# The last group of a four-layer graph network: where its copies and activations run, and how its last rows are written

## The chip, the core and the metric

The kernel runs on one core of one Trainium2 chip. A core has TensorE (PE, with its weight loads shown as PEld), VectorE (DVE), ScalarE (ACT), GpSimd (POOL), SyncE (SP, which only issues transfers here) and 16 DMA engines. Each engine takes its own instructions in order; they wait for each other by semaphores. The metric is the device time of one execution in microseconds, the median of several runs. All arithmetic is in float32.

## The reference, cut to what matters

The input is 128 graphs of 64 nodes with 512 features: `x` (128, 64, 512), `adj` (128, 64, 64), and a node mask. Four layers follow one another, each as `x = layernorm(x + layer(x))`:

```python
# layer 0: hypergraph convolution twice, with H = (adj != 0) and row weights Dn, Be
m   = Be * (H^T @ (x @ W^T));   conv = Dn * (H @ m) + b
h   = layer_norm(relu(conv(x, W1, b1))) * gamma + beta;   y = conv(h, W2, b2) + x
# layer 1: a rank-one attention
s   = (x @ w) @ a;   A = s[i] + s[j];   A = tanh(A / 8) * 8;   A = where(A >= 0, A, 0.1 * A)
A   = exp(A) * adj;  A = A / A.sum(-1) * adj.sum(-1);   y = A @ x @ w
# layer 2: three graph convolutions
x1  = relu(adj @ (x @ W1) + b1);   x2 = relu(adj @ (x1 @ W2) + b2);   y = adj @ (x2 @ W3) + b3
# layer 3: attention with 8 heads of 64, plus terms in adj
attn = softmax(masked(q @ k^T / 8)) * 0.33 + 0.33 * adj + 0.33 * exp(-adj)   # under the mask
y   = (attn @ v) @ W_out + b_out
```

The output is `x` after layer 3.

## The kernel before

**Tiling.** Two graphs make a *pair* of 128 rows, two pairs a *duo*, and four pairs a *group* of 512 rows: the 8192 rows are 16 groups. A group's features sit in `xg` (128 partitions, 4 pairs, 512). Where a product needs features on the partitions, the group is held transposed in a `Left` (128, 4 chunks, 512 rows).

**Products.** `multiply` computes a 512x512x512 product in four quadrants from seven products of half size instead of eight. `Left.sums` makes the three sums or differences of quadrants that this takes on the left side (DVE, L518 to L521). The seven products (`product`, all recorded as L539) accumulate in three tiles named `a_...`, `b_...` and `c_...`. Between them ACT copies intermediate sums away (`snap`, L555), DVE adds quadrants together (L575, L581, L590), and ACT copies the last quadrant (L600). `rows_of` is the plain product for one pair, written to a tile `pp`; it is used by the first group, and by the last one for the output projection. Accumulators come from `ps_acc` (4 banks), all other PSUM tiles (`gth`, `xtp`, `ptp`, `agg`) from `ps_gt` (4 banks).

**Order.** The lists `start`, `order`, `step_1`, `step_last` and `rest_last` at the end of the kernel give the order of the stages. In the steady part three groups are interleaved: `a` (layers 0 and 1) of one group, `b` (layer 2 and the scores of layer 3) of the group before, `t` (the rest of layer 3) of the one before that. In `step_last` only `b` of the last group (q = 15, `NGRP - 1`) and `t` of group 14 are left, and in `rest_last` only `t` of the last group, `last_rows`. Within this order a scheduler places the instructions of each engine; `behind(key)` keeps an instruction after a named one, `in_turn(engine)` after the newest one of that engine. In `rest_last` PE and DVE are kept strictly in the written order (those instructions are recorded under L127, the helper's line).

**The last group's stages, in order of time.**

- `l2a`: the first layer-2 product. Its quadrants land in `h1` (named `aT_h` in the profile); the relu with bias is L1081 (by quadrants, in `relu`, group 0) or L1089 (by chunks of 128x512, all later groups). `pv` of group 14 (L1376) and its copies `taken` (L1388, to `aT_oT`) fall between `l2a` and `l2b`.
- `l2b`, then `gth` (L1112), which multiplies with the adjacency and leaves `h2` transposed in four `ps_gt` banks; eight relus (L1120) bring it to SBUF. `shifted` adds the bias `gb3` to `xg` (L737) and makes the masks (`prepare_masks`, L719 to L730) on DVE. Then `h2.sums()` and `l2c`.
- the aggregation `agg` (L1145), a layer norm, and `xtp` (L1165), which transposes `xg` into PSUM; four copies (L1170) bring it to `aT_xT`, and the products `q`, `k` follow.
- `last_rows`: softmax steps, `ptp` (the probabilities transposed), `pv`, `taken`, and for each pair `projected` (the product `pp`), `added` (to `xg`), `layer_norm` and a write. Pair 3 is done in two halves of 256 columns in one PSUM tile. Writes are issued by SP (L1262 for pairs 0 to 2, L1288 for pair 3).

Weights stream through a ring of 20 tiles, issued by SP as places come free.

Of the kernel before, what the change touches and what calls it, by code (L numbers as in the profile page):

```python
# [8 lines left out]
FP = mybir.dt.float32  # L9
U8 = mybir.dt.uint8  # L10
AF = mybir.ActivationFunctionType
ALU = mybir.AluOpType
AX = mybir.AxisListType

P = 128
C = 64
D = 512
# [4 lines left out]
KD = D // P  # L22
Q = 256
# [3 lines left out]
LA = LD = LG = 0.33  # L27
# [14 lines left out]
def kernel(  # L42
# [28 lines left out]
    nc = tc.nc  # L71
    NT = x.shape[0]
    NPAIR = NT // P
    NGRP = NPAIR // G
# [370 lines left out]
    def rstd(mv, n, key, at=slice(None)):  # L445
        rs = small.tile([P, n], FP, name=f"rs_{key}", tag="rs")
        act.activation(rs[:, at], mv[:, at, 1], AF.Sqrt, bias=eps_t)  # L447
        vec.reciprocal(rs[:, at], rs[:, at])
        return rs
# [48 lines left out]
    def newest(engine):  # L498
        return next(i for i in reversed(nc.cur_bb.bb.instructions) if i.engine == engine)
# [112 lines left out]
    def turned(t):  # L612

        return lambda m, n: t[:, 2 * n : 2 * n + 2, m * Q : (m + 1) * Q]
# [118 lines left out]
    def shifted(g, key):  # L733

        with behind(key):
            for p in range(G):
                vec.tensor_add(g["x"][:, p, :], g["x"][:, p, :], gb3_bc)  # L737
            prepare_masks(g)
# [147 lines left out]

    def rows_of(p, ts, quads, u0=0, u1=None, ps=None, ns=range(2)):

        if ps is None:
            ps = ps_acc.tile([P, 2, Q], FP, name=f"pp_{p}", tag="acc")  # L890
        us = range(len(ts))[u0:u1]
        for n in ns:
            for u in us:
                for c in range(KD):
                    ten.matmul(
                        ps[:, n, :], ts[u][:, c, p * P : (p + 1) * P], quads[u][c // 2, n][:, c % 2],
                        start=(n == 0 and u == 0 and c == 0), stop=(u == len(ts) - 1 and c == KD - 1),
                        skip_group_check=True,
                    )
        return ps  # L900
# [162 lines left out]
    def second_half(g):  # L1063
# [18 lines left out]
                    turned(h1.t)(m, n)[:, c], src[:, c], AF.Relu, bias=gb1_col[:, 2 * n + c : 2 * n + c + 1]  # L1082
                )

        for _ in multiply([left], (w_g[0], q), turned(h1.t), f"l2a_{q}", flipped=True, then=relu if q == 0 else None):
            yield "l2a1"
        if q > 0:
            for c in range(KD):
                act.activation(h1.t[:, c, :], h1.t[:, c, :], AF.Relu, bias=gb1_col[:, c : c + 1])  # L1089
        h1.sums()  # L1090
# [5 lines left out]
        adt = grp.tile([P, G, C], FP, name=f"adt_{q}", tag="adt", bufs=1)  # L1096
        act.activation(adt, g["atc"], AF.Exp, scale=-1.0)
        g["adt"] = adt
        if alone:
            shifted(g, f"l2b_{q}")  # L1100
        yield "gb3"

# [2 lines left out]
        for c2 in range(2):  # L1105
            ps = [ps_gt.tile([P, 2, G, C], FP, name=f"gth2_{q}_{c2}_{h}", tag="gt") for h in range(2)]
            for c in range(2):
                for p in range(G):
                    for f in range(2):
                        for h in range(2):  # L1110
                            rows, c0 = slice(h * C, (h + 1) * C), (2 * c2 + c) * P + f * C
                            ten.matmul(  # L1112
                                ps[h][f * C : (f + 1) * C, c, p, :],
                                g2[rows, p, c0 : c0 + C], g["atc"][rows, p, :], start=True, stop=True,
                            )
            for c in range(2):
                k = 2 * c2 + c
                o = h2.t[:, k, :].rearrange("p (d h t) -> p d h t", d=2, h=2)
                for h in range(2):
                    act.activation(  # L1120
                        o[:, :, h, :], ps[h][:, c].rearrange("p (d a) i -> p d (a i)", d=2),
                        AF.Relu, bias=gb2_col[:, k : k + 1],
                    )
        if not alone:
            shifted(g, f"l0w2_{q + 1}.u2")
        h2.sums()
        yield "gh"
        g3 = big.tile([P, G, D], FP, name=f"g3_{q}", tag="big")
        gen = multiply([h2], (w_g[2], q), nat(g3), f"l2c_{q}", stops=(3, 5),
# [28 lines left out]
        for duo in range(2):  # L1158
            ps = [ps_gt.tile([P, KD, 2, C], FP, name=f"xtp_{q}_{duo}_{h}", tag="gt") for h in range(2)]
            for c in range(KD):  # L1160
                for p in range(2):
                    for h in range(2):
                        rows = slice(h * C, (h + 1) * C)
                        with behind("l1w_1.p6") if q == 0 else nullcontext():
                            ten.transpose(  # L1165
                                ps[h][:, c, p, :], xg[rows, 2 * duo + p, c * P : (c + 1) * P], identc[rows]
                            )
            o = left.t[:, :, duo * Q : (duo + 1) * Q].rearrange("p c (a g i) -> p c a g i", a=2, g=2)
            for h in range(2):
                act.copy(o[:, :, :, h, :], ps[h])  # L1170
        left.sums()
        yield "xT"
        qT = big.tile([P, KD, T], FP, name=f"qT_{q}", tag="big")
# [50 lines left out]
    def last_rows(g, probs, v, left):  # L1224

        q, xg = g["q"], g["x"]
        o = out[q * T : (q + 1) * T, :].rearrange("(p t) d -> t p d", t=P)
        gen = multiply([left], (w_v, q), nat(v), f"v_{q}", stops=(3, 6))
        next(gen)
        yield "v1"  # L1230
        steps = [[softmax_steps(g, duo, probs[duo], h2) for h2 in range(2)] for duo in range(2)]
        for n in range(2):
            for h2 in range(2):
                next(steps[0][h2])
        for n in range(2):
            next(steps[1][0])
        for h2 in range(2):
            next(steps[0][h2])
        next(gen)
        yield "v2"  # L1240
        left = Left(f"oT_{q}")
        pts = turn_probs(g, 0, probs[0])
        whole(gen)
        yield "v"
        taken(0, attend(g, 0, pts, v), left)
        for n in range(2):
            next(steps[1][1])
        for h2 in range(2):
            next(steps[1][h2])
        yield "pv0"  # L1250

        def projected(p, ps=None, n=None):
            return rows_of(p, [left.t], stream.here[w_o, q], ps=ps, ns=range(2) if n is None else (n,))

        def added(p, ps, n=None):
            cols = slice(0, D) if n is None else slice(n * Q, (n + 1) * Q)
            row = xg[:, p, cols]
            vec.tensor_add(row, ps.rearrange("p n f -> p (n f)")[:, cols], row)

        def written(p):  # L1260
            layer_norm(xg, f"l3_{q}_{p}", (p,))
            nc.sync.dma_start(out=o[:, p], in_=xg[:, p])  # L1262

        ps = projected(0)
        pts = turn_probs(g, 1, probs[1])
        added(0, ps)
        written(0)
        yield "o1"
        ps = projected(1, n=0)
        taken(1, attend(g, 1, pts, v), left)  # L1270
        ps = projected(1, ps, n=1)
        added(1, ps)
        written(1)
        yield "pv1"
        added(2, projected(2))
        written(2)

        st = small.tile([P, 2, 6], FP, name="st_last", tag="st_last", bufs=1)
        ps = None
        for n in range(2):  # L1280
            ps = projected(3, ps, n=n)
            added(3, ps, n)
            vec.bn_stats(st[:, n], xg[:, 3, n * Q : (n + 1) * Q])
        mv = small.tile([P, 1, 2], FP, name="mv_last", tag="mv_last", bufs=1)
        vec.bn_aggr(mv[:, 0, :], st.rearrange("p n s -> p (n s)"))
        rs = rstd(mv, 1, "last")
        vec.tensor_scalar(xg[:, 3], xg[:, 3], mv[:, 0, 0:1], rs[:, 0:1], ALU.subtract, ALU.mult)
        nc.sync.dma_start(out=o[:, 3], in_=xg[:, 3])  # L1288
        yield "o"

    def softmax_steps(g, duo, ds, h2):
# [73 lines left out]
    def attend(g, duo, pts, v):  # L1365

        q = g["q"]

        ps = [ps_acc.tile([P, 4, 2, C], FP, name=f"pv_{q}_{duo}_{gg}", tag="acc") for gg in range(2)]
        for hc in range(4):  # L1370
            for p in range(2):
                for h2 in range(2):
                    hd = 2 * hc + h2
                    for gg in range(2):
                        rows = slice(gg * C, (gg + 1) * C)
                        ten.matmul(  # L1376
                            ps[gg][h2 * C : (h2 + 1) * C, hc, p, :],
                            v[rows, 2 * duo + p, hd * C : (hd + 1) * C],
                            pts[p][rows, h2 * 4 + hc, :],
                            start=True,  # L1380
                            stop=True,
                        )
        return ps

    def taken(duo, ps, left):
        o4 = left.t[:, :, duo * Q : (duo + 1) * Q].rearrange("p c (a g i) -> p c a g i", a=2, g=2)
        for gg in range(2):
            act.mul(o4[:, :, :, gg, :], ps[gg], LA)  # L1388

# [174 lines left out]
```

## Time and profile before

| | |
|---|---|
| median of 3 runs | 2749.85 us (2749.43 to 2751.62) |
| the profiled execution | 2749.3 us |
| its span, first to last instruction | 2747.5 us |
| granted TensorE clock, mean | 0.999 of full speed |
| busy: PE, DVE, ACT, POOL | 2722.5, 2079.6, 803.3, 38.1 us |
| last group alone (`rest_last`, from the first v product at 2708.8) | 38.7 us |
| longest kinds of wait on ACT | for DVE's statistics: 244.2 us in 44 waits |

An idle engine costs time only where the chain that ends last passes through it. So the head of the page says which engine carries that chain, the chain of waits says where it leaves that engine, and the timeline around such a place says which instruction was late. The profiled execution is one of many; its durations are read from it, and its own time is set beside the median of the runs.

### The profile page before, as it was taken

Reading aid. Unit: us, or ns where it says so; the run is one execution under the profiler, and the core shown is the slowest. Engines: PE = TensorE matmul, PEld = TensorE weight load, DVE = VectorE, ACT = ScalarE, POOL = GpSimd, SP = SyncE. Lnnn points to the kernel's source line nnn. Section 1 sums busy time; section 2 is a strip of 40 time slices with the busy share of each in tenths; the row PEclk is TensorE's granted clock in tenths of the full one; section 3 lists DMA queues with packets and bytes.
Section 4 is the critical chain, followed back from the end, with each engine's and each line's share of the span. In section 5 each row is a group of like instructions: output and inputs, shape, how many; then the busy total and the mean of one; then the engine's idle time right before and its main releaser. Section 6 shows DMA issues by size and latency. Waiting matters only on the chain.

```text
span 2747.5 us, 67717 instructions
## 1 busy us (share of the span) xinstructions
PE 2722.5 (99%) x28770; PEld 2347.5 (85%) x28770; DVE 2079.6 (76%) x4117; ACT 803.3 (29%) x1444; POOL 38.1 (1%) x71
## 2 busy tenths in 40 slices
PE   9999999999999999999999999999999999999998
PEld 7878888888888888888888888888888888888887
DVE  6878687776877778777786877778777687776766
ACT  3323323233232322322223232232322323232232
POOL 2000000000000000000000000000000000000000
PEclk9999999999999999999999999999999999999999
DMA  8535454454544545445454454545545455454441
GB/s 264 179 107 164 129 166 140 141 165 131 171 132 138 167 132 165 131 143 167 130 167 131 143 165 131 165 126 153 159 131 170 129 159 147 130 163 132 151 124 61
DMA packets 309388, 405.14 MB, mean 147 GB/s; under 512 B 57408, under 2 KB 185184, under 8 KB 309088
## 3 DMA queue, kind: packets, MB, share of 16 engines
q1 hardware_dynamic: 304256, 385.58, 47.5%
q0 software_dynamic: 4832, 15.24, 1.5%
q8 instruction: 228, 3.74, 0.6%
q14 instruction: 72, 0.59, 0.1%
HBM read 369.78 MB, written 30.93 MB: 146 GB/s over the span
## 4 chain that ended last, share of the span: by engine, by line
PE 88%; DVE 10%; ACT 1%; issue 1%; POOL 0%; DVEq 0%; POOLq 0%
PE a_l0w L539 13%; PE b_l0w L539 7%; PE a_l2b L539 4%; PE a_q L539 4%; PE a_k L539 4%; PE a_l2a L539 4%; PE a_v L539 4%; PE c_l0w L539 4%; PE a_l1w L539 4%; PE gt_l L481 3%; PE a_wo L539 3%; PE gt_l0h L481 2%; PE a_l2c L539 2%; PE b_l2b L539 2%; PE b_q L539 2%; PE b_k L539 2%
## 5 line engine op out<-in xcount | busy, mean ns | idle before, releaser
L539 PE MATMUL a_l0w<-w2w,aT_l0h 128*128 128x256 f32 x720 | 164.3, 381 | 0.0
L457 DVE BATCH_NORM_STATS2 st_l<-x 128x6 f32<-128x512 f32 x244 | 157.4, 671 | 0.6
L539 PEld LDWEIGHTS a_l0w<-w2w,aT_l0h 128*128 128x128 f32 x720 | 135.6, 190 | 18.8
L463 DVE TENSOR_SCALAR x<-x,mv_l,rs_l 128x512 f32<-128x512 f32 x244 | 119.2, 541 | 2.2
L539 PE MATMUL b_l0w<-w2w,s_l0h 128*128 128x256 f32 x480 | 108.5, 379 | 0.0
L771 ACT ACTIVATE h<-h 128x1024 f32<-128x1024 f32 (+1 forms) x58 | 54.9, 947 | 178.5 <-DVE h L590 157.5
L539 PEld LDWEIGHTS b_l0w<-w2w,s_l0h 128*128 128x128 f32 x480 | 91.1, 190 | 12.5
L1120 ACT ACTIVATE aT_h<-gth,gb_col 128x256 f32<-128x256 f32 x128 | 48.4, 489 | 159.0 <-PE gth L1112 159.0
L492 ACT COPY aT_l<-gt_l 128x512 f32<-128x512 f32 x148 | 78.1, 597 | 56.8 <-PE gt_l L481 56.8
L447 ACT ACTIVATE rs_l<-mv_l,eps_t 128x4 f32<-128x4 f32 (+1 forms) x64 | 19.0, 297 | 255.9 <-DVE mv_l L458 244.2
L555 DVE TENSOR_TENSOR u_l0w<-a_l0w,b_bc 128x512 f32<-128x512 f32 x56 | 38.6, 688 | 69.3 <-PE a_l0w L539 69.3
L539 PE MATMUL a_l2c<-gwcw,aT_h 128*128 128x256 f32 x360 | 86.7, 384 | 4.2 <-ACT u_l2c L555 3.2
L539 PE MATMUL a_l2b<-gwbw,aT_h 128*128 128x256 f32 x360 | 86.6, 383 | 0.7 <-ACT aT_oT L1388 0.7
L539 PE MATMUL a_q<-aT_xT,wqw 128*128 128x256 f32 x360 | 85.1, 379 | 0.6 <-ACT aT_xT L1170 0.6
L539 PE MATMUL a_l1w<-ww,aT_l 128*128 128x256 f32 x360 | 85.1, 379 | 0.2 <-ACT aT_l L492 0.2
L539 PE MATMUL a_k<-aT_xT,wkw 128*128 128x256 f32 x360 | 85.0, 379 | 0.0
L539 PE MATMUL a_l2a<-aT_l,gwaw 128*128 128x256 f32 x360 | 85.0, 379 | 0.0
L539 PEld LDWEIGHTS a_l2c<-gwcw,aT_h 128*128 128x128 f32 x360 | 67.0, 190 | 18.7 <-ACT u_l2c L555 8.7
L539 PE MATMUL a_v<-wvw,aT_xT 128*128 128x256 f32 x336 | 80.8, 383 | 0.0
L539 PE MATMUL a_l0w<-w1aw,aT_l 128*128 128x256 f32 x336 | 80.8, 383 | 0.0
L539 PE MATMUL a_wo<-wow,aT_oT 128*128 128x256 f32 x336 | 79.5, 379 | 0.1
L539 PE MATMUL a_l0w<-w1bw,aT_l 128*128 128x256 f32 x336 | 79.4, 379 | 0.0
(528 smaller groups left out, 6486.9 us busy)
## 6 DMA issues: line engine op xcount, KB each, us to landing
w2w<-w2k SPq DMA_DIRECT2D x210, 256.0 KB, 2.6
x<-in_x_dram SPq DMA_DIRECT2D x15, 1024.0 KB, 9.8
w1aw<-w1ak SPq DMA_DIRECT2D x60, 256.0 KB, 2.7
w1bw<-w1bk SPq DMA_DIRECT2D x60, 256.0 KB, 2.7
ww<-wk SPq DMA_DIRECT2D x60, 256.0 KB, 2.8
gwaw<-gwak SPq DMA_DIRECT2D x60, 256.0 KB, 3.1
gwbw<-gwbk SPq DMA_DIRECT2D x60, 256.0 KB, 2.6
gwcw<-gwck SPq DMA_DIRECT2D x60, 256.0 KB, 2.7
```

The lines of the kernel that those rows point to most:

```text
L447: act.activation(rs[:, at], mv[:, at, 1], AF.Sqrt, bias=eps_t)
L457: vec.bn_stats(st, xg[:, p, :])
L463: vec.tensor_scalar(xg[:, p, :], xg[:, p, :], mv[:, p, 0:1], rs[:, p : p + 1], ALU.subtract, ALU.mult)
L481: ten.matmul(ps[g][f * C : (f + 1) * C, c, p, :], src(2 * duo + p)[rows, c0 : c0 + C], mat[rows, 2 * duo + p, :], start=True, stop=True,)
L492: act.copy(o[:, :, :, g, :], ps[g])
L539: ten.matmul(acc[:, blk, :], lhsT, rhs, start=(first and blk == 0 and i == 0), stop=(last and i == n_k - 1), skip_group_check=True,)
L555: last_add[f"{key}.{what}"] = (act.copy(t, ps) if res is None else vec.tensor_add(t, ps, res(m, n))).ins
L771: act.activation(hn, hn, AF.Relu)
L1120: act.activation(o[:, :, h, :], ps[h][:, c].rearrange("p (d a) i -> p d (a i)", d=2), AF.Relu, bias=gb2_col[:, k : k + 1],)
```

## The change

All of it acts on the last group only (`q == NGRP - 1`).

- The relus of `l2a` go by quadrants, as in group 0; the last quadrant goes from PSUM through the relu without a copy of its own.
- Of the eight relus of `gth`, the four with h = 1 go to DVE as a `tensor_scalar` (add, max). `h2.sums()` comes before `shifted`.
- Of the four copies of the transposed x, two go to DVE.
- For duo 0 of `pv`, one of the two copies goes to DVE, and both come before the next softmax step. That step is split: its maximum comes before them, the subtraction and the exponential after.
- Pair 3 has a PSUM tile for each half, and both halves are multiplied at once. The statistics of pair 2 and pair 3 are written out by hand: the add and statistics of half 0 stand before the reciprocal of pair 2. Pair 3 is scaled and written in two halves, the first issued by SP, the second by ACT.

```diff
--- before.py
+++ after.py
@@ -886,7 +886,8 @@
 
     def rows_of(p, ts, quads, u0=0, u1=None, ps=None, ns=range(2)):
 
-        if ps is None:
+        fresh = ps is None
+        if fresh:
             ps = ps_acc.tile([P, 2, Q], FP, name=f"pp_{p}", tag="acc")
         us = range(len(ts))[u0:u1]
         for n in ns:
@@ -894,7 +895,7 @@
                 for c in range(KD):
                     ten.matmul(
                         ps[:, n, :], ts[u][:, c, p * P : (p + 1) * P], quads[u][c // 2, n][:, c % 2],
-                        start=(n == 0 and u == 0 and c == 0), stop=(u == len(ts) - 1 and c == KD - 1),
+                        start=(fresh and n == ns[0] and u == 0 and c == 0), stop=(u == len(ts) - 1 and c == KD - 1),
                         skip_group_check=True,
                     )
         return ps
@@ -1082,9 +1083,9 @@
                     turned(h1.t)(m, n)[:, c], src[:, c], AF.Relu, bias=gb1_col[:, 2 * n + c : 2 * n + c + 1]
                 )
 
-        for _ in multiply([left], (w_g[0], q), turned(h1.t), f"l2a_{q}", flipped=True, then=relu if q == 0 else None):
+        for _ in multiply([left], (w_g[0], q), turned(h1.t), f"l2a_{q}", flipped=True, then=relu if alone else None):
             yield "l2a1"
-        if q > 0:
+        if not alone:
             for c in range(KD):
                 act.activation(h1.t[:, c, :], h1.t[:, c, :], AF.Relu, bias=gb1_col[:, c : c + 1])
         h1.sums()
@@ -1096,7 +1097,7 @@
         adt = grp.tile([P, G, C], FP, name=f"adt_{q}", tag="adt", bufs=1)
         act.activation(adt, g["atc"], AF.Exp, scale=-1.0)
         g["adt"] = adt
-        if alone:
+        if q == 0:
             shifted(g, f"l2b_{q}")
         yield "gb3"
 
@@ -1117,13 +1118,17 @@
                 k = 2 * c2 + c
                 o = h2.t[:, k, :].rearrange("p (d h t) -> p d h t", d=2, h=2)
                 for h in range(2):
-                    act.activation(
-                        o[:, :, h, :], ps[h][:, c].rearrange("p (d a) i -> p d (a i)", d=2),
-                        AF.Relu, bias=gb2_col[:, k : k + 1],
-                    )
+                    cols = ps[h][:, c].rearrange("p (d a) i -> p d (a i)", d=2)
+                    if q == NGRP - 1 and h == 1:
+                        vec.tensor_scalar(o[:, :, h, :], cols, gb2_col[:, k : k + 1], 0.0, ALU.add, ALU.max)
+                    else:
+                        act.activation(o[:, :, h, :], cols, AF.Relu, bias=gb2_col[:, k : k + 1])
         if not alone:
             shifted(g, f"l0w2_{q + 1}.u2")
         h2.sums()
+        if q == NGRP - 1:
+            last_add["h2s"] = newest(DVE)
+            shifted(g, "h2s")
         yield "gh"
         g3 = big.tile([P, G, D], FP, name=f"g3_{q}", tag="big")
         gen = multiply([h2], (w_g[2], q), nat(g3), f"l2c_{q}", stops=(3, 5),
@@ -1167,7 +1172,10 @@
                             )
             o = left.t[:, :, duo * Q : (duo + 1) * Q].rearrange("p c (a g i) -> p c a g i", a=2, g=2)
             for h in range(2):
-                act.copy(o[:, :, :, h, :], ps[h])
+                if q == NGRP - 1 and h == 1:
+                    vec.tensor_copy(o[:, :, :, h, :], ps[h])
+                else:
+                    act.copy(o[:, :, :, h, :], ps[h])
         left.sums()
         yield "xT"
         qT = big.tile([P, KD, T], FP, name=f"qT_{q}", tag="big")
@@ -1242,8 +1250,10 @@
         pts = turn_probs(g, 0, probs[0])
         whole(gen)
         yield "v"
-        taken(0, attend(g, 0, pts, v), left)
-        for n in range(2):
+        next(steps[1][1])
+        with in_turn(ACT):
+            taken(0, attend(g, 0, pts, v), left, both=True)
+        with in_turn(ACT):
             next(steps[1][1])
         for h2 in range(2):
             next(steps[1][h2])
@@ -1252,14 +1262,21 @@
         def projected(p, ps=None, n=None):
             return rows_of(p, [left.t], stream.here[w_o, q], ps=ps, ns=range(2) if n is None else (n,))
 
-        def added(p, ps, n=None):
-            cols = slice(0, D) if n is None else slice(n * Q, (n + 1) * Q)
-            row = xg[:, p, cols]
-            vec.tensor_add(row, ps.rearrange("p n f -> p (n f)")[:, cols], row)
+        def added(p, ps):
+            row = xg[:, p]
+            vec.tensor_add(row, ps.rearrange("p n f -> p (n f)"), row)
 
         def written(p):
             layer_norm(xg, f"l3_{q}_{p}", (p,))
             nc.sync.dma_start(out=o[:, p], in_=xg[:, p])
+
+
+        st = small.tile([P, 2, 6], FP, name="st_last", tag="st_last", bufs=1)
+
+        def half(n, ps):
+            row = xg[:, 3, n * Q : (n + 1) * Q]
+            vec.tensor_add(row, ps[:, n], row)
+            vec.bn_stats(st[:, n], row)
 
         ps = projected(0)
         pts = turn_probs(g, 1, probs[1])
@@ -1273,19 +1290,27 @@
         written(1)
         yield "pv1"
         added(2, projected(2))
-        written(2)
-
-        st = small.tile([P, 2, 6], FP, name="st_last", tag="st_last", bufs=1)
-        ps = None
+        ps = [projected(3, n=n) for n in range(2)]
+        mv = small.tile([P, 2, 2], FP, name="mv_last", tag="mv_last", bufs=1)
+        s2 = small.tile([P, 6], FP, name="st_last2", tag="st", bufs=4)
+        vec.bn_stats(s2, xg[:, 2])
+        vec.bn_aggr(mv[:, 0, :], s2)
+        rs = small.tile([P, 2], FP, name="rs_last", tag="rs_last", bufs=1)
+        act.activation(rs[:, 0:1], mv[:, 0:1, 1], AF.Sqrt, bias=eps_t)
+        half(0, ps[0])
+        vec.reciprocal(rs[:, 0:1], rs[:, 0:1])
+        vec.tensor_scalar(xg[:, 2], xg[:, 2], mv[:, 0, 0:1], rs[:, 0:1], ALU.subtract, ALU.mult)
+        nc.sync.dma_start(out=o[:, 2], in_=xg[:, 2])
+        half(1, ps[1])
+        vec.bn_aggr(mv[:, 1, :], st.rearrange("p n s -> p (n s)"))
+        act.activation(rs[:, 1:2], mv[:, 1:2, 1], AF.Sqrt, bias=eps_t)
+        vec.reciprocal(rs[:, 1:2], rs[:, 1:2])
         for n in range(2):
-            ps = projected(3, ps, n=n)
-            added(3, ps, n)
-            vec.bn_stats(st[:, n], xg[:, 3, n * Q : (n + 1) * Q])
-        mv = small.tile([P, 1, 2], FP, name="mv_last", tag="mv_last", bufs=1)
-        vec.bn_aggr(mv[:, 0, :], st.rearrange("p n s -> p (n s)"))
-        rs = rstd(mv, 1, "last")
-        vec.tensor_scalar(xg[:, 3], xg[:, 3], mv[:, 0, 0:1], rs[:, 0:1], ALU.subtract, ALU.mult)
-        nc.sync.dma_start(out=o[:, 3], in_=xg[:, 3])
+            cols = slice(n * Q, (n + 1) * Q)
+            vec.tensor_scalar(
+                xg[:, 3, cols], xg[:, 3, cols], mv[:, 1, 0:1], rs[:, 1:2], ALU.subtract, ALU.mult
+            )
+            (nc.sync, nc.scalar)[n].dma_start(out=o[:, 3, cols], in_=xg[:, 3, cols])
         yield "o"
 
     def softmax_steps(g, duo, ds, h2):
@@ -1382,10 +1407,13 @@
                         )
         return ps
 
-    def taken(duo, ps, left):
+    def taken(duo, ps, left, both=False):
         o4 = left.t[:, :, duo * Q : (duo + 1) * Q].rearrange("p c (a g i) -> p c a g i", a=2, g=2)
         for gg in range(2):
-            act.mul(o4[:, :, :, gg, :], ps[gg], LA)
+            if both and gg == 1:
+                vec.tensor_scalar_mul(o4[:, :, :, gg, :], ps[gg], LA)
+            else:
+                act.mul(o4[:, :, :, gg, :], ps[gg], LA)
 
 
 
```

## The prediction

> **What bounds the kernel now.** I read first the page's head, the share of each engine:
>
> ```profile
> span 2747.5 us, 67717 instructions
> PE 2722.5 (99%) x28770; PEld 2347.5 (85%) x28770; DVE 2079.6 (76%) x4117; ACT 803.3 (29%) x1444; POOL 38.1 (1%) x71
> ```
>
> TensorE is busy all the time and its clock is full (0.999 granted). Whatever the change does to DVE or ACT can pay only where TensorE stands still. In the steady groups another group's products fill every wait; the last group has no such partner. So I read the chain of waits from 2560 us on, and then the timeline around each pause of TensorE in it. Columns: start, duration, engine, line, what; in brackets the idle time before it and its releaser.
>
> ```profile
> 2634.87 2.12 PE L1376 MATMUL pv<-pt,v 64*64 64x64 f32 x128
> 2635.81 1.33 ACT L1089 ACTIVATE aT_h<-aT_h,gb_col 128x512 f32<-128x512 f32 x2
> 2637.05 1.06 ACT L1388 ACTIVATE aT_oT<-pv 128x512 f32<-128x512 f32 x2
> 2637.68 1.99 PE L539 MATMUL a_l2b<-gwbw,aT_h 128*128 128x256 f32 x8 [0.69 <-ACT aT_oT L1388]
> ...
> 2651.69 3.02 ACT L1120 ACTIVATE aT_h<-gth,gb_col 128x256 f32<-128x256 f32 x8 [1.03 <-PE gth L1112]
> 2654.74 0.69 DVE L518 TENSOR_TENSOR s_h<-aT_h 128x512 f32<-128x512 f32 x1 [1.64 <-ACT aT_h L1120]
> 2655.54 1.97 PE L539 MATMUL b_l2c<-gwcw,s_h 128*128 128x256 f32 x8 [1.03 <-issue]
> ...
> 2681.29 2.05 ACT L1170 COPY aT_xT<-xtp 128x512 f32<-128x512 f32 x4 [5.69 <-PE xtp L1165]
> 2682.41 1.99 PE L539 MATMUL a_q<-aT_xT,wqw 128*128 128x256 f32 x8 [0.65 <-ACT aT_xT L1170]
> 2683.38 0.69 DVE L518 TENSOR_TENSOR s_xT<-aT_xT 128x512 f32<-128x512 f32 x1 [2.03 <-ACT aT_xT L1170]
> ...
> 2722.76 0.63 ACT L1298 ACTIVATE sm<-sm 128x512 f32<-128x512 f32 x1
> 2723.29 1.06 ACT L1388 ACTIVATE aT_oT<-pv 128x512 f32<-128x512 f32 x2
> 2724.41 3.72 PE L127 MATMUL pp<-wob,aT_oT 128*128 128x256 f32 x16 [1.31 <-ACT aT_oT L1388]
> ...
> 2739.86 0.41 DVE L127 TENSOR_TENSOR x<-pp,x 128x256 f32<-128x256 f32 x1
> 2740.33 1.99 PE L127 MATMUL pp<-wob,aT_oT 128*128 128x256 f32 x8 [1.44 <-DVE x L127]
> 2742.37 0.42 DVE L127 TENSOR_TENSOR x<-pp,x 128x256 f32<-128x256 f32 x1 [1.62 <-PE pp L127]
> 2744.06 0.55 DVE L127 TENSOR_SCALAR x<-x,mv_last,rs_last 128x512 f32<-128x512 f32 x1
> 2744.63 0.33 SPq L1288 DMA_DIRECT2D out_dram<-x  x1
> ```
>
> Five seams. A: l2b's first product waits for an accumulator that the oldest pv copy must free, and that copy queues on ACT behind the relus. B: the second product waits for the sum s_h, and that for ACT's eighth relu. C: ACT copies both halves of the transposed x alone. D: two pv copies queue behind an exponential; the next product (pp) waits 1.3 us. E: the last half product waits for an add that DVE reaches late, and then the end follows.
>
> The chip's measurement can tell about 0.2% from no change here, 5.5 us.
>
> **The change part by part.** Compared instruction by instruction, both programs are the same on all queues until A; SP's and POOL's order changes nowhere but in the last write. What an earlier seam gains is carried on, because the later waits follow TensorE's own results, and weights are issued long ahead (those of pp at 2686, used at 2724).
>
> *A.* Removed: four relus of 128x512 and the copy before two of them; added: eight of 128x256, six as each quadrant arrives. Price: the gth rows of that size, 0.49 each at a pace of 0.36. The last two read the accumulator when the product ends (2634.94), so 2634.98 + 0.36 + 0.49 = 2635.83. The pv half is complete at about 2636.1; the copy takes 0.59, to 2636.7. pv itself ends its issue at 2634.87 + 2.02 = 2636.89, so TensorE no longer stops: 2637.68 - 2636.89 = **0.8**. The second pv pair reuses the accumulator that these relus read and could wait 0.1; bounds 0.5 to 0.8.
>
> *B.* Removed from ACT: four of eight relus, now on DVE. DVE has no row of this operation from PSUM; bounds 0.28 (`neg`, a tensor_scalar of 128x256 from SBUF) and 0.42 (an add of 128x256). I take 0.41; ACT's 0.49 is longer anyway. gth's second bank is complete at 2652.6; ACT then does its two: 2652.66 + 0.36 + 0.49 = 2653.5. The sum starts 1.2 earlier than 2654.74; TensorE, done with the first product at 2652.50 + 1.73 = 2654.23, would start at 2653.55 + 0.80 = 2654.35 instead of 2655.54: **1.2** (0.9 to 1.25). Moved back on DVE to after the sums: the x shift and masks (4 x 0.6 and five of about 0.35: 4.1 us). They end near 2660.2. Queued behind is the add of c_l2c, due at 2659.6, with nobody waiting before the aggregation at 2667.8: 7 us of cover.
>
> *C.* Two of four copies to DVE. DVE's copy of this form (L490) takes 0.692, ACT's 0.597. DVE is free at 2681.30 (behind the add of a_wo), so 2681.99 instead of 2682.41, and s_xT, now started at 2682.63, removes the 0.1 before b_q: **0.5** (0.3 to 0.6).
>
> *D.* One copy goes to DVE, and ACT's comes before the exponential. pv ends at 2723.09, ACT at 2723.7. For DVE two rows compete: a tensor_scalar of 128x512 takes 0.541 (L463, from SBUF), a copy from PSUM 0.692. The Trainium skill, "VectorE: DVE Perf Modes", section "Why PSUM operands drop a tier", says that DVE has one PSUM read port, so a PSUM operand of fp32 runs at 1x. By L463 pp starts at 2723.7, a gain of 0.7; by the rule, with the PSUM row, at 2723.86: **0.55** (0.3 to 0.7). The rule is against the change, and I take it. Behind the waiting DVE instruction stand a subtraction, then the exponential, two sums and two scalings, 3.8 us in a row (2722.03 to 2725.84). They now end at about 2727.6; their reader, the second half of the transposes, comes at 2723.86 + 3.65 + 0.33 = 2727.84. Cover 0.25; beyond it every delay costs itself. On ACT the table load for the square roots (1.28, at 2724.37 before) follows the exponential and now ends near 2726.4; the first root after it comes at 2731.1, so it stays hidden.
>
> *E.* A bank of its own for each half: the second half follows at once, so TensorE ends at 2738.89 + 1.73 = 2740.62 instead of 2742.32. Is DVE ready? Add and statistics of pair 2, then half 0 at 2738.93 (0.45 + 0.36), reciprocal, scale: 2740.5. So the last add starts at 2740.67, 1.7 earlier. From it to the scale is 1.69 as before; two half scales (0.28, 0.21 apart) put the issues at 2742.65 (SP) and 2742.87 (ACT), the later 1.76 earlier. For the write itself, the table by stretches (busy time of each engine, clock, DMA share, GB/s) shows when data moves:
>
> ```profile
> 2745.00:2745.40 0.40, 0.00 (x0) 0.00 (x0) 0.00 (x0) 0.00 (x0) 0.00 (x0) 1.00 0.00 0
> 2745.40:2745.80 0.40, 0.00 (x0) 0.00 (x0) 0.00 (x0) 0.00 (x0) 0.00 (x0) 1.00 0.81 307
> 2745.80:2746.20 0.40, 0.00 (x0) 0.00 (x0) 0.00 (x0) 0.00 (x0) 0.00 (x0) 1.00 0.91 343
> 2746.20:2746.60 0.40, 0.00 (x0) 0.00 (x0) 0.00 (x0) 0.00 (x0) 0.00 (x0) 1.00 0.02 5
> ```
>
> Of the 2.87 us from 2744.63 to the end it moves for 0.8. Two rules bear on it. "DMA: Bandwidth & Descriptors", section "Anatomy of one DMA", gives a fixed 2.0 us plus bytes over 436 GB/s: half the bytes save an estimated 0.3. Section "Issuing engines are not separate DMA queues" says that another issuer buys only issue time: so the second half queues behind the first half's rest, and of the 0.4 that the row would give (half of 0.8), 0.2 remains. Unhidden is the first DMA ever issued by ACT, which no row shows: by SP's writes (2.0 us to landing, median) it costs nothing more; by POOL's of 256 KB (2.6 to 10.6) up to 8. I take SP's row, the nearest. So E gives 1.76 + 0.2 = **2.0** (1.2 to 2.3, ACT's queue aside).
>
> Sum: 0.8 + 1.2 + 0.5 + 0.55 + 2.0 = 5.0 us, off a profiled execution of 2749.3 (span 2747.5, 1.8 around it): 2744.3. The median of the runs, 2749.85, is 0.55 above that execution; I set the forecast against it: 2744.85, 0.18% less.
>
> **The rivals.** *R1, over the bound* (28%): the seams reach their upper ends, 0.8 + 1.25 + 0.6 + 0.7 + 2.3 = 5.65, so 2744.2. For it: in A TensorE cannot do better, but DVE's prices in B and D are my higher ones. Against it: all five must be near their ends; chance of the medians (2749.43 to 2751.62) helps it more than the profile.
>
> *R2, the seams move on* (15%): DVE becomes the late engine. In C and D its copies sit behind other work, the 0.25 cover of D is used up, and the half-row writes save nothing. Lower bounds 0.5 + 0.9 + 0.3 + 0.3 + 1.2 = 3.2: 2746.65.
>
> *R3, slower* (5%): ACT's own queue is slow at its first use. Issued at 2742.87 - 3.05 = 2739.8 (A to D before it), with 0.9 from landing to the end of the span: the change loses once the landing takes over 6.8 us. With POOL's worst row, 10.6, the span ends at 2751.3, 3.8 later: 2753.6. A loss of over 0.2% takes 12.3. Against it: ACT's queue is none of POOL's, and its wait is for DVE only.
>
> The forecast itself (gain 4.0 to 5.5) has 52%. That leaves 28% for faster by over 0.2%, 69% within and 3% slower. The range takes the forecast's case, R1's end with half a microsecond for the medians, and R2 to its middle: 2743.4 to 2746.8.
>
> **What would show it.** After: no idle of TensorE before a_l2b; b_l2c within 0.2 of a_l2c's end; a_q released by DVE 0.7 after the transposes' first half; pp released by DVE's pv copy, and no new idle before the following transposes; 40 pp records in one run; the last DMA issued some 4.8 us earlier than 2744.63 and the span ending 2.7 after it. I am wrong if TensorE idles before those transposes, if the ACT write lands later than 2.4 us, or if DVE's add of half 1 starts after its product's end.

## The result, and the profile after

| | before | changed |
|---|---|---|
| median of 20 runs | 2749.81 us (2747.81 to 2751.62) | 2745.15 us (2744.3 to 2747.43) |
| ratio, with its 95% interval | | 0.9984 (0.9978 to 0.9991) |
| span of the profiled execution | 2747.5 us | 2743.1 us |

The change makes the kernel faster by 4.7 us by the medians; the interval of the ratio reaches from 2.5 to 6.0 us. That is less than the 5.5 us which the prediction took for the least that can be told from no change; with 20 runs of each kernel this gain can be told from none. 2744.85 had been forecast. The page's head is nearly unchanged, as it should be when 4 us of standing still go from 2747:

```profile
span 2743.1 us, 67728 instructions
PE 2721.8 (99%) x28770; PEld 2351.5 (86%) x28770; DVE 2083.8 (76%) x4125; ACT 801.3 (29%) x1440; POOL 38.1 (1%) x71
```

The same places of the timeline as in the prediction, now of the changed kernel (start, duration, engine, line, what; in brackets the idle time before and its releaser):

```profile
2634.34 2.15 PE L1401 MATMUL pv<-pt,v 64*64 64x64 f32 x128
2634.45 0.84 ACT L1082 ACTIVATE aT_h<-a_l2a,gb_col 128x256 f32<-128x256 f32 x2
2635.55 2.07 ACT L1416 ACTIVATE aT_oT<-pv 128x512 f32<-128x512 f32 x4 [0.27 <-PE pv L1401]
2636.42 2.00 PE L539 MATMUL a_l2b<-gwbw,aT_h 128*128 128x256 f32 x8
...
2650.43 1.75 ACT L1125 ACTIVATE aT_h<-gth,gb_col 128x256 f32<-128x256 f32 x4 [1.03 <-PE gth L1113]
2650.48 1.79 DVE L1123 TENSOR_SCALAR aT_h<-gth,gb_col 128x256 f32<-128x256 f32 x4 [2.70 <-PE gth L1113]
2652.37 0.69 DVE L518 TENSOR_TENSOR s_h<-aT_h 128x512 f32<-128x512 f32 x1
2653.16 1.97 PE L539 MATMUL b_l2c<-gwcw,s_h 128*128 128x256 f32 x8
...
2678.92 1.09 ACT L1178 COPY aT_xT<-xtp 128x512 f32<-128x512 f32 x2 [5.69 <-PE xtp L1170]
2678.95 1.29 DVE L1176 COPY aT_xT<-xtp 128x512 f32<-128x512 f32 x2
2679.75 1.97 PE L539 MATMUL a_q<-aT_xT,wqw 128*128 128x256 f32 x8 [0.35 <-ACT aT_xT L1178]
...
2720.49 0.69 DVE L127 TENSOR_SCALAR aT_oT<-pv 128x512 f32<-128x512 f32 x1 [1.19 <-PE pv L127]
2721.28 3.69 PE L127 MATMUL pp<-wob,aT_oT 128*128 128x256 f32 x16 [0.89 <-ACT aT_oT L1416]
...
2728.57 8.90 PE L127 MATMUL pp<-wob,aT_oT 128*128 128x256 f32 x40
2737.51 0.42 DVE L127 TENSOR_TENSOR x<-pp,x 128x256 f32<-128x256 f32 x1 [0.20 <-PE pp L127]
2739.20 0.73 DVE L127 TENSOR_SCALAR x<-x,mv_last,rs_last 128x256 f32<-128x256 f32 x2
2739.64 0.33 SPq L1313 DMA_DIRECT2D out_dram<-x  x1
2739.96 0.37 ACTq L1313 DMA_DIRECT2D out_dram<-x  x1
```

Most of the predicted marks are there: no idle time stands before a_l2b, four relus run on each engine at once, and the last products are one run of 40. Two are missed. The last write is issued 4.67 us earlier (2744.63 to 2739.96), and 0.53 of that is the earlier start of A, so 4.14 where 4.8 was set; and the span ends 3.09 after that issue, not 2.7. The bracket before a_q and pp names ACT, although the DVE copy ended later (2678.95 + 0.69 = 2679.64 and 2720.49 + 0.69 = 2721.18, each about 0.1 before TensorE starts); the views put a wait for two semaphores down to one of them.

Absolute times of two executions can't be subtracted here. Up to seam A both kernels hold the same instructions, and yet the first pv matmul of group 14 starts at 2634.87 before and at 2634.34 after; over the 14 profiled executions of this study it lies between 2633.73 and 2638.72. The profiles drift apart by steps of up to 1.8 us in differing groups; the cause stays open. So I measured each of the seams A to D from TensorE's first matmul of one product to its first matmul of the next, from the starts in the trace, and E in three pieces. Over all kernels that share a seam these lengths repeat within 0.03 us.

| seam, from ... to | before | changed | gain | forecast |
|---|---|---|---|---|
| A: pv of group 14 to a_l2b | 2.81 | 2.08 | 0.73 | 0.8 |
| B: gth to b_l2c | 5.57 | 4.46 | 1.11 | 1.2 |
| C: xtp to a_q, and a_q to b_q | 1.87 + 1.83 | 1.57 + 1.80 | 0.33 | 0.5 |
| D: pv to pp, and pp to ptp | 2.47 + 3.65 | 2.05 + 3.62 | 0.45 | 0.55 |
| E: pv of duo 1 to the last add | 11.74 | 10.03 | 1.71 | 1.7 |
| E: from the (first) scale to the last landing | 2.58 | 2.52 | 0.06 | 0.25 |
| E: from the last landing to the end of the span | 0.90 | 1.34 | -0.44 | 0 |

The gains add up to 3.95 us, not 5.0, and the earlier start of A (0.53) makes up the rest of the 4.5 us between the two spans (2747.54 and 2743.05). The stretches between the seams are the same to 0.01.

### The profile page after: what moved, and what is told of

Read it like the earlier page. It is cut to its first block, busy times and chain, and to the rows that moved or that the text cites. A ratio compares the mean times of both kernels' runs of the same rounds, so it can differ in the third digit from the quotient of the medians.

```text
span 2743.1 us, 67728 instructions
## 1 busy us (share of the span) xinstructions
PE 2721.8 (99%) x28770; PEld 2351.5 (86%) x28770; DVE 2083.8 (76%) x4125; ACT 801.3 (29%) x1440; POOL 38.1 (1%) x71
## 4 chain that ended last, share of the span: by engine, by line
PE 88%; DVE 10%; ACT 1%; issue 0%; DMA 0%; DVEq 0%
PE a_l0w L539 13%; PE b_l0w L539 7%; PE a_l2b L539 4%; PE a_q L539 4%; PE a_k L539 4%; PE a_l2a L539 4%; PE a_v L539 4%; PE c_l0w L539 4%; PE a_l1w L539 4%; PE gt_l L481 3%; PE a_wo L539 3%; PE gt_l0h L481 2%; PE a_l2c L539 2%; PE b_l2b L539 2%; PE b_k L539 2%; PE b_q L539 2%
## 5 line engine op out<-in xcount | busy, mean ns | idle before, releaser
L463 DVE TENSOR_SCALAR x<-x,mv_l,rs_l 128x512 f32<-128x512 f32 x244 | 119.2, 542 | 2.2
```

Source lines behind the costliest of these rows:

```text
L463: vec.tensor_scalar(xg[:, p, :], xg[:, p, :], mv[:, p, 0:1], rs[:, p : p + 1], ALU.subtract, ALU.mult)
```

## The experiments

Each kernel is the changed one with one edit. All but x_lanes were run once; their times (2744.09 to 2750.02) mean nothing at this size, and it is the seams in their traces that answer. The theory behind the first group (S in the expectations: what counts is when SP checks the last write's semaphore; its rival Q is that ACT's queue costs time at the end) came from the last row of the table. (Two of the expectations put the 1.34 of that row at 1.39 and at 1.35 to 1.4; the trace's own landing gives 1.34.) At the end SP checks ten semaphores one after another, 0.061 us each. The views don't print these checks; in the trace their starts are:

```
before  2745.01 2745.06 2745.12 2745.19 2745.25 2745.31 2745.37 2745.43 2745.49 | 2746.66        last landing 2746.64
changed 2740.01 2740.07 | 2741.73 2741.80 2741.86 2741.92 2741.98 2742.04 2742.10 2742.16        last landing 2741.72
```

Eight of the ten belong to the DMA semaphores, which the transfers use in rotation, numbered 0 to 7. Before, the last write was on 7, the last to be checked. In the changed kernel one transfer more moves it to 0, the third check, and seven checks come after its landing.

**x_lanes**: one transfer fewer, so that the last two writes are on 6 and 7.

```diff
             layer_norm(xg, f"l3_{q}_{p}", (p,))
-            nc.sync.dma_start(out=o[:, p], in_=xg[:, p])
+            if p == 1:
+                nc.sync.dma_start(out=o[:, 0:2], in_=xg[:, 0:2])
```

> The writes of pairs 0 and 1 become one, so the two half writes of pair 3 move by one place in the rotation of the eight DMA semaphores, from places 7 and 0 to 6 and 7. In the changed kernel 1.39 us pass from the last landing to the end of the span, against 0.90 before. Theory S (SP checks the eight semaphores one after another at the end, and the last write sits early in that row, so the rest of the checks come after it): back to 0.90, the part from the last issue to the end 2.65 instead of 3.14. Theory Q (a second queue, ACT's, costs time at the end): stays at 1.4. The whole: 0.5 less than the changed kernel under S, which the medians can't tell; against the kernel before 0.9982 to 0.9986 either way.

From the last landing to the end it takes 0.91 us. The changed kernel's loss of 0.44 is won back in the trace. The medians are too coarse for it: against the kernel before, the ratio is 0.9985 (0.9979 to 0.9992), which can't be told from the changed kernel's.

**x_spboth**: both halves issued by SP.

```diff
-            (nc.sync, nc.scalar)[n].dma_start(out=o[:, 3, cols], in_=xg[:, 3, cols])
+            (nc.sync, nc.sync)[n].dma_start(out=o[:, 3, cols], in_=xg[:, 3, cols])
```

> Both half writes are issued by SP, on the same two semaphore places 7 and 0 as in the changed kernel; ACT issues none. Theory S: from the last landing to the end again 1.35 to 1.4, since the place is what counts. Theory Q: 0.90, as no second queue is in use. The second issue comes 0 to 0.1 later than ACT's; landing 1.7 to 1.8 after it.

It takes 1.34 us again, so it is the place and not ACT's queue. SP's second issue begins 0.87 us after the first scale, ACT's 0.77.

**x_place3**: pair 0 written in four transfers, so that ACT's write is on place 3.

```diff
             layer_norm(xg, f"l3_{q}_{p}", (p,))
-            nc.sync.dma_start(out=o[:, p], in_=xg[:, p])
+            for r in range(4 if p == 0 else 1):
+                rows = slice(32 * r, 32 * r + 32) if p == 0 else slice(0, P)
+                nc.sync.dma_start(out=o[rows, p], in_=xg[rows, p])
```

> Pair 0 is written in four transfers of 32 rows, so that the last write (ACT's) sits on semaphore place 3 of 0 to 7; all else as changed. Theory S, with one check each 0.061 us: from the last landing to the end 0.90 at place 7, 1.34 at place 0, so 1.34 - 3 x 0.061 = 1.16 here. Theory Q (the queue counts): 1.34. The four small writes are over long before.

It takes 1.15 us. With seven, four and no checks left after that of the last write, the stretch is 1.34, 1.15 and 0.90 us, a line of 0.06 a check. So the order of the checks is settled as the cause.

**x_onewrite**: pair 3 scaled and written in one piece.

```diff
-        for n in range(2):
-            cols = slice(n * Q, (n + 1) * Q)
-            vec.tensor_scalar(
-                xg[:, 3, cols], xg[:, 3, cols], mv[:, 1, 0:1], rs[:, 1:2], ALU.subtract, ALU.mult
-            )
-            (nc.sync, nc.scalar)[n].dma_start(out=o[:, 3, cols], in_=xg[:, 3, cols])
+        vec.tensor_scalar(xg[:, 3], xg[:, 3], mv[:, 1, 0:1], rs[:, 1:2], ALU.subtract, ALU.mult)
+        nc.sync.dma_start(out=o[:, 3], in_=xg[:, 3])
```

> Pair 3 is scaled in one piece and written by SP in one transfer on semaphore place 7, as before the change; all else as changed. From the start of the (first) scale to the end of the span the changed kernel takes 3.9 us. If the half scales and half writes bring what I forecast (0.2 from the bytes), this is about 0.2 to 0.4 slower, 4.1 or more. If what the trace suggests holds (half scales of 0.41 each where 0.28 was priced, and theory S), it is faster: 0.57 to the issue, 2.01 to landing, 0.90 to the end, 3.5 in all.

```profile
2740.06 0.55 DVE L127 TENSOR_SCALAR x<-x,mv_last,rs_last 128x512 f32<-128x512 f32 x1
2740.63 0.33 SPq L1309 DMA_DIRECT2D out_dram<-x  x1
```

From the scale to the landing it takes 2.59 us, and to the end 3.50, against 2.52 + 1.34 = 3.86 in the changed kernel: the halved write as it was placed loses 0.36. With the places right (x_lanes, 2.52 + 0.91 = 3.43) it wins about 0.06, by one trace of each.

**x_onebank**: one PSUM tile for both halves.

```diff
-        ps = [projected(3, n=n) for n in range(2)]
+        ps3 = projected(3, n=0)
...
-        half(0, ps[0])
+        half(0, ps3)
+        projected(3, ps3, n=1)
...
-        half(1, ps[1])
+        half(1, ps3)
```

> Both halves of pair 3 in one PSUM tile again, the statistics in their new places. If the bank is what the gain of the last product rests on (theory B), TensorE stops before the second half until the add of half 0 has read its bank: that add now comes 0.8 earlier than in the kernel before, so of the 1.7 us between the two versions about 0.85 is lost. If the places of the statistics alone carry it (theory P), nothing is lost. If they carry nothing, all of 1.7 is lost.

```profile
2740.17 0.42 DVE L127 TENSOR_TENSOR x<-pp,x 128x256 f32<-128x256 f32 x1
2740.65 1.99 PE L127 MATMUL pp<-wob,aT_oT 128*128 128x256 f32 x8 [0.52 <-DVE x L127]
2742.68 0.42 DVE L127 TENSOR_TENSOR x<-pp,x 128x256 f32<-128x256 f32 x1 [0.98 <-PE pp L127]
```

TensorE stops again until DVE's add has read half 0; from pv of duo 1 to the last add it takes 10.81, so 0.78 of the 1.71 is lost. Whether the shared tile or the bank under it makes TensorE wait, no run separates.

**x_oldplaces**: two banks, but half 0's add and statistics behind the scaling of pair 2.

```diff
         act.activation(rs[:, 0:1], mv[:, 0:1, 1], AF.Sqrt, bias=eps_t)
-        half(0, ps[0])
         vec.reciprocal(rs[:, 0:1], rs[:, 0:1])
...
+        half(0, ps[0])
         half(1, ps[1])
```

> A bank for each half, but the add and statistics of half 0 again after pair 2 is scaled. If the bank alone carries the gain, the last add comes as in the changed kernel, 10.03 after the first pp of the last run of products, or up to 0.15 later, as DVE finishes half 0's statistics at about the time when TensorE finishes half 1. If the places matter as much as the bank, 10.8.

```profile
2737.36 0.42 DVE L127 TENSOR_TENSOR x<-pp,x 128x256 f32<-128x256 f32 x1
2737.81 0.43 DVE L127 BATCH_NORM_STATS2 st_last<-x 128x6 f32<-128x256 f32 x1
2738.16 0.42 DVE L127 TENSOR_TENSOR x<-pp,x 128x256 f32<-128x256 f32 x1
```

It takes 10.03, counted as in the table from pv of duo 1 (the expectation calls that start the first pp; from the pp itself it is 8.94). Nothing is lost: DVE goes from half 0 to half 1 without a pause, at just the time when the product is done. With a tile for each half the places of the statistics are worth nothing; with one tile they are worth the 0.93 that x_onebank keeps.

**x_undoA**: the relus of l2a by chunks again.

```diff
-..., then=relu if alone else None):
+..., then=relu if q == 0 else None):
...
-        if not alone:
+        if q > 0:
             for c in range(KD):
                 act.activation(h1.t[:, c, :], h1.t[:, c, :], AF.Relu, bias=gb1_col[:, c : c + 1])
```

> The relus of l2a by chunks of 128x512 again, with the copy before them; all else as changed. If the gain at A comes from the pv copy that no longer queues behind long relus, the time from the first pv matmul of group 14 to the first l2b matmul goes back from 2.08 to 2.8 (before: 2.81). If it comes from ACT being freed by something else in the change, it stays at 2.1. The other seams keep their lengths to 0.05.

A is 2.81 again, all other seams keep their lengths within 0.02. The new form of the relus carries the whole of it.

**x_undoBrelu**, all eight relus of gth on ACT:

```diff
-                    if q == NGRP - 1 and h == 1:
+                    if False:
                         vec.tensor_scalar(o[:, :, h, :], cols, gb2_col[:, k : k + 1], 0.0, ALU.add, ALU.max)
```

**x_undoBorder**, the shift and the masks before the sums again:

```diff
-        if q == 0:
+        if alone:
             shifted(g, f"l2b_{q}")
...
-        if q == NGRP - 1:
-            last_add["h2s"] = newest(DVE)
-            shifted(g, "h2s")
```

> All eight relus of gth on ACT again, h2.sums() still before the shift. The time from the first gth matmul to the first b_l2c matmul is 5.57 before and 4.46 changed. If the split over two engines carries it, 5.5 to 5.6 here; if the earlier place of the sums carries it, 4.5.

> The relus split over ACT and DVE, but the shift of x and the masks before them again on DVE, as in the kernel before. DVE then has 4.1 us of work that begins right after the last l2b add, about 1.2 before gth. If the order matters as much as I think (DVE's relus queue behind that work), gth to b_l2c is 6.3 to 6.9, longer than before; if the relus can pass it, 4.5.

B takes 5.58 and 5.49, against 5.57 before: neither half of the edit does much by itself. In x_undoBorder DVE comes to its relus late:

```profile
2652.22 1.75 ACT L1125 ACTIVATE aT_h<-gth,gb_col 128x256 f32<-128x256 f32 x4 [1.03 <-PE gth L1113]
2653.10 0.48 DVE L1123 TENSOR_SCALAR aT_h<-gth,gb_col 128x256 f32<-128x256 f32 x1
2653.49 0.41 DVE L730 TENSOR_TENSOR adt<-adt,m 128x256 f32<-128x256 f32 x1
2653.83 1.26 DVE L1123 TENSOR_SCALAR aT_h<-gth,gb_col 128x256 f32<-128x256 f32 x3
```

I had expected this one to be 6.3 or more. The work ahead of the relus (2649.49 to 2653.91 in this trace) is mostly done while gth is still multiplied, and the scheduler lets one relu pass the last of it. So it ends 0.09 better than before, not 0.7 worse.

**x_undoC**: all four copies of the transposed x on ACT.

```diff
-                if q == NGRP - 1 and h == 1:
+                if False:
                     vec.tensor_copy(o[:, :, :, h, :], ps[h])
```

> All four copies of the transposed x on ACT again. From the first transpose to the first a_q matmul: 1.87 before, 1.57 changed, where I had forecast 1.45. Back to 1.87, and a_q to b_q from 1.80 to 1.83, so 0.33 in all. If the missing 0.1 is the hand-over from DVE to TensorE (copy ends 0.11 before the matmul starts), here with ACT as the releaser it is 0.05.

C takes 1.87 and 1.83, as before the change, and a_q starts 0.05 after ACT's second copy ends, as expected.

**x_undoD**: the pv copies as before the change; **x_orderD**: only the second of the two copies back on ACT, the order kept.

```diff
# x_undoD
-        next(steps[1][1])
-        with in_turn(ACT):
-            taken(0, attend(g, 0, pts, v), left, both=True)
-        with in_turn(ACT):
-            next(steps[1][1])
+        taken(0, attend(g, 0, pts, v), left)
+        for n in range(2):
+            next(steps[1][1])
# x_orderD
         with in_turn(ACT):
-            taken(0, attend(g, 0, pts, v), left, both=True)
+            taken(0, attend(g, 0, pts, v), left, both=False)
```

> The pv copies of duo 0 both on ACT and behind the exponential again. From the first pv matmul to the first pp matmul: 2.47 before, 2.05 changed, 1.93 forecast. Back to 2.47 here, and the transposes after pp 3.65 after its start (changed: 3.62).

> The new order is kept (copies before the exponential), but both copies are on ACT. If the order carries the gain at D, pv to pp is near 2.05; if the split over two engines does, near 2.47. By the rows I expect between: ACT's two copies take 1.06 from 1.21 after pv's start, so pp at 2.33: order 0.14, split 0.28. No new wait before the transposes, since the exponential comes only 0.4 later.

From pv to pp it takes 2.47 in x_undoD and 2.35 in x_orderD, near the 2.33 expected:

```profile
2720.28 1.08 ACT L1416 ACTIVATE aT_oT<-pv 128x512 f32<-128x512 f32 x2 [0.52 <-PE pv L127]
2721.24 0.63 ACT L1323 ACTIVATE sm<-sm 128x512 f32<-128x512 f32 x1
2721.41 1.16 PEld L127 LDWEIGHTS pp<-wob,aT_oT 128*128 128x128 f32 x6 [1.33 <-ACT aT_oT L1416]
```

So the order alone is worth 0.12, the split over two engines the other 0.30. TensorE starts 0.05 after ACT's second copy here; in the changed kernel it starts 0.10 after DVE's.

## Why the prediction was right, and where not

- **What bounds it** held: all gains lie where TensorE stood still, and each was carried on to the end.
- **A** (0.8, measured 0.73): the mechanism is shown by x_undoA. The 0.1 that the second pv pair might wait is there in part: pv takes 2.15 instead of 2.12.
- **B** (1.2, measured 1.11): the mis-sized term is DVE's relu from PSUM. I took 0.41 between bounds of 0.28 and 0.42; its four took 0.475 to 0.485, so both bounds were too low and DVE, not ACT, ended last. The cover for the moved shift (7 us) was ample. That order and split pay only together came from the experiments; the sum had one figure for both.
- **C** (0.5, measured 0.33): DVE's copy took 0.69 as taken from L490. Two terms were wrong. I left out the hand-over from DVE to TensorE: a_q starts 0.10 after the copy ends. And I counted 0.1 for a pause before b_q that was never there. The first line is the kernel before, beside the sum s_xT that the prediction shows (2683.38 + 0.69 = 2684.07); the other two are the changed one:

```profile
2684.25 1.89 PE L539 MATMUL b_q<-s_xT,wqw 128*128 128x256 f32 x8
...
2680.34 0.69 DVE L518 TENSOR_TENSOR s_xT<-aT_xT 128x512 f32<-128x512 f32 x1
2681.55 1.89 PE L539 MATMUL b_q<-s_xT,wqw 128*128 128x256 f32 x8
```

  The sum is done 0.18 before b_q in the old kernel and 0.51 before it in the new one, and in both b_q's first matmul follows a_q's last by 0.216, the pace within a_q. The 0.03 that a_q to b_q did shorten (1.83 to 1.80) lies between a_q's first two matmuls.
- **D** (0.55, measured 0.45): the rule of the Trainium skill that I weighed ("VectorE: DVE Perf Modes", "Why PSUM operands drop a tier") agrees: the tensor_scalar from PSUM took 0.69, not the 0.54 of the row from SBUF. The missing 0.1 is the same hand-over, 0.10, and a start 0.02 later than set, less 0.03 behind pp. The cover of 0.25 before the transposes held: they start 3.62 after pp, with no new wait.
- **E** (2.0, measured 1.33): the last add came 1.71 earlier, forecast 1.70. Two terms of the rest failed. The half scale was priced at 0.28 after a tensor_scalar with constants; with its two operands per partition it takes 0.41, so the last issue came 0.77 after the first scale's start instead of 0.51. Two rows of the kernel before have the same operands and would have given it: 0.541 for 512 columns (L463) and 0.810 for 1024 (L785) lie on a line that makes an estimated 0.41 for 256. And the path from landing to the end, which I took over unchanged, grew by 0.44. The write itself took 1.75 from ACT's issue to landing instead of 2.01: 0.26 for the 0.2 forecast. Of the two rules of the Trainium skill ("DMA: Bandwidth & Descriptors"), the fit in "Anatomy of one DMA" is given there for transfers that GpSimd issues, and these are not: for 256 KB it makes an estimated 2.6, where 2.01 was measured, and only its difference for half the bytes, an estimated 0.3, is near. The rule of "Issuing engines are not separate DMA queues" held: ACT's issue comes 0.10 earlier than SP's second one in x_spboth, and lands 1.75 after it where SP's takes 1.77.
- **R1** would have needed all five seams at their upper ends; none reached it. **R2** came true in part, and its sum, 3.2, is nearer to the 3.95 than my 5.0: DVE was the later engine at B, C and D, by about 0.1 each, and the halved write cost more than it saved; but D's cover was not used up. **R3** did not happen: the first write on ACT's queue landed in 1.75 us, no later than SP's in the same place.

The median lies 0.3 us from the forecast, but 3.95 us is what the seams show, just under the 4.0 to 5.5 of the forecast's own case. Taken off the median before, it makes 2745.9, inside the stated range and 1.0 from the forecast. So the places and the order of the gains were foreseen, and the closeness of the median is mostly luck. The difference between 3.95 and the medians' 4.7 is within the interval, and the varying time ahead of seam A (5 us from end to end over 14 executions) is large enough for it. Two sums of the prediction are loose: its five terms make 5.05, not 5.0, and R1's end less half a microsecond is 2743.7, not 2743.4. Neither changes the outcome.

## What to carry to other kernels

At the end of a kernel with no partner work, list TensorE's pauses, and price each edit from the last engine that releases it, with the hand-over. Before splitting a copy over two engines, see that the second engine's queue is clear of other work: at B the split without the reordering gained 0.09 of 1.11, and the reordering without the split nothing. When the number of transfers changes, see on which semaphore the last write falls and in which order the end of the program waits for them.

## What the runs showed of the hardware that I had not expected

- SP's checks at the end of the program take 0.061 us each, in the same order in all 14 traces: 0.90, 1.15 and 1.34 us from the last landing to the end for the last write on semaphore 7, 3 and 0.
- DVE's tensor_scalar of 128x256 took 0.28 with constants (SBUF), 0.41 with two operands per partition (SBUF), and 0.48 from PSUM with one such operand. No run changes the operands alone.
- TensorE starts 0.10 us after a DVE copy has ended and 0.05 after one of ACT (seams C and D). Its second matmul follows 0.29 after the first behind DVE and 0.32 behind ACT, so that most of the difference is gone by then.
- The last write of 256 KB landed 2.01 us after its issue; its halves took 1.71 and 1.75 us.
